# A two-layer graph attention kernel: the first stage's work dealt out anew over the engines

## The chip, the cores and the metric

The kernel runs on one core of a Trainium2 chip. The metric is the device time of one execution in microseconds (us), as the median of several runs. Five engines work side by side, each through its own queue of instructions in program order, and wait for each other by semaphores: TensorE (PE in the profile; PEld is its weight loads), VectorE (DVE), ScalarE (ACT), GpSimd (POOL) and SyncE (SP). SP and POOL here mostly issue DMAs.

## The reference

Two graph attention layers over 512 nodes, a residual and a layer norm. There are 16,896 edges (8,192 drawn ones, the same reversed, and a loop at each node), sorted by destination. Layer 1 has 8 heads of 768 features, layer 2 has one.

```python
def gat_layer(x, W, a_s, a_d, b, edge_index, concat):
    h = (x @ W).reshape(n, H, C)
    alpha_s = jnp.einsum('nhc,hc->nh', h, a_s)
    alpha_d = jnp.einsum('nhc,hc->nh', h, a_d)
    e = jax.nn.leaky_relu(alpha_s[src] + alpha_d[dst], 0.2)
    m = jax.ops.segment_max(e, dst, num_segments=n)
    e = jnp.exp(e - m[dst])
    denom = jax.ops.segment_sum(e, dst, num_segments=n)
    alpha = e / (denom[dst] + 1e-16)
    out = jax.ops.segment_sum(h[src] * alpha[:, :, None], dst, num_segments=n)
    return out.reshape(n, H * C) + b

h = elu(gat_layer(x, W1, a_src1, a_dst1, b1, edge_index, True))
y = gat_layer(h, W2, a_src2, a_dst2, b2, edge_index, True)
return layernorm(x + y)
```

## The kernel before

The edges become a dense matrix `cnt` of 512 by 512 (how often an edge runs from a source to a destination), in 4 tiles of 128 destinations. Each head is then dense: a projection of x, logits, a softmax of each tile over all 512 sources with the counts as weights, attention, ELU, and a product with the head's rows of W2 added into `h2`.

**The large products** are made of fewer, smaller ones (Strassen's way, by halves): seven products P1 to P7 of sums and differences of blocks, each in two parts i = 0, 1 with three steps each (`product`, L422). `left(xT, xS)` (L401) gives the sums of the transposed x: `s1` to `s4` on VectorE (L406 to L409). The weights' sums of head 0 are made by `weight_sums` (L554): one VectorE addition, `w1t` (L556), which P5 reads, and then accumulating DMAs of GpSimd: `t2 += t1` (L261), which P6 reads, one into `w1r` (L558), which P7 reads, and `t4 += t2` (L262), which P4 reads. The same function loads the weights of head 1 and makes their sums.

**The first stage** (not `general`, from L700) counts the edges beside the projection of head 0 (`first_projection`, L601, 14 items) and the first four items of head 1's (`projection`). The edges are in 132 chunks of 128. For each chunk a one-hot tile of its sources is made, on VectorE (L753) or, for tile 2 of the destinations, on ScalarE (L751); for each quarter of the chunks VectorE makes the destinations' side (`here`, `odw`, L731, L732); TensorE multiplies the two (L779) into one PSUM bank a tile. Sources are folded in half, and the counts of the two halves lie in one number as digits; `counted_in_digits` (L578) takes them apart: `higher` (ScalarE: `upper` and a half of `cnt`), `lower` (VectorE, the other half), `mask` (ScalarE, `absent`, from `cnt`).

The order is written out by hand. `batches` (L815) deals the chunks into nine batches, as pairs of numbers: so many of the other tiles' chunks, so many of tile 2's. In each batch VectorE gets the destinations of new quarters, then the one-hots, with what is `waiting` in their middle; then come the `extra` steps (L809), then the projection's items up to `wants[n]`, then the batch's counting. An item's addition on VectorE is put into `waiting`, and so comes in the middle of the next batch's one-hots. `logits(0, ...)` makes both halves of a tile's logits (L441): with the source vector `a_s`, then with the destination vector `a_d`.

In the last batch `spread` (L649) transposes and broadcasts the source logits of head 0 on TensorE. A tile's softmax steps are `lift` (ScalarE: logit sum, L669), `leak` (VectorE, L673), `rank` (VectorE: mask and maximum, L678; ScalarE: exponential, L684), then `give`: `weigh` (VectorE: L936 to L940), scale and a copy on ScalarE (L956, L959), a transposing DMA on SP (L961), and `turn_in` (ScalarE, L964) into `PT`.

**The rest of head 1's projection** is a loop over `pairs[4]` to `pairs[13]`, two each for P6, P7, P4, P5 and P3; P4 accumulates into P7's bank and waits for P7's addition (L465), P3 likewise into P5's. What is put between them stands in `beside` (L1158): the rest of head 0's softmax, `done[n]`, which empties a pair, and sums. `load_a(1)` loads head 1's two vectors into the tiles of head 0's.

**Head 0's attention** is `near_first` (L1056, matmuls L1067), whose last argument says which steps come beside which product, among them halves of head 1's logits and `row_out(1)` (DVE, then DMAs through DRAM that broadcast the source logits). Then follows `by_halves(h2, ...)`, head 0's part of the second layer, with the softmax of head 1 beside it. Heads 1 to 7 aren't touched otherwise.

Of the kernel before, what the change touches and what calls it, by code (L numbers as in the profile page):

```python
# [39 lines left out]
def gat_pass(  # L40
# [393 lines left out]
    def half_logits(h, t):  # L434
        return [lambda al=al, a=a, sign=sign: nc.vector.scalar_tensor_tensor(
            scr, HS[h][:, t, :], sign, a, op0=ALU.mult, op1=ALU.mult, accum_out=al[:, t:t + 1])
            for al, a, sign in zip(AL[h], A[h], (1.0, -1.0))]

    def logits(h, feats, t):
        for al, a, sign in zip(AL[h], A[h], (1.0, -1.0)):  # L440
            nc.vector.scalar_tensor_tensor(scr, feats[:, t, :], sign, a, op0=ALU.mult,  # L441
                                           op1=ALU.mult, accum_out=al[:, t:t + 1])
# [135 lines left out]
    def counted_in_digits(t, ps, steps):  # L578

        both = ps[:, :HN]  # L580
        if steps:
            st = ohp.tile([P, HN + 1], F32, name="steps")
            nc.scalar.activation(st[:, 1:], both, AF.Copy, scale=0.5)
            nc.scalar.activation(st[:, :1], ps[:, HN - 1:HN], AF.Copy, scale=-0.5)
            both = ohp.tile([P, HN], F32, name="both")
            nc.vector.tensor_tensor(both, st[:, 1:], st[:, :HN], op=ALU.subtract)
        upper = ohp.tile([P, HN], F32, name="upper", bufs=2)

        def higher():
            nc.scalar.activation(upper, both, AF.Identity, bias=minus_round, scale=-1.0)  # L590
            nc.scalar.activation(cnt[:, t, HN:], upper, AF.Copy, bias=-ROUND / DIGIT, scale=-1.0 / DIGIT)

        def lower():
            nc.vector.scalar_tensor_tensor(cnt[:, t, :HN], upper, ROUND, both, op0=ALU.add, op1=ALU.add)

        def mask():
            nc.scalar.activation(absent[:, t, :], cnt[:, t, :], AF.Relu, bias=far, scale=NO_EDGE)

        return higher, lower, mask
# [72 lines left out]
    def leak(q):  # L672
        nc.vector.scalar_tensor_tensor(q, q, NEG_SLOPE, q, op0=ALU.mult, op1=ALU.min)  # L673
# [37 lines left out]
    if not general:  # L711
# [46 lines left out]
        def sources(chunks, between):  # L758

            for j, c in enumerate(chunks):  # L760
                if j == len(chunks) // 2:
                    for f in between:
                        f()
                one_hot(c, False)
# [3 lines left out]
        def count(batch, rest):  # L768
# [14 lines left out]
            for t in range(NT):  # L783
                if t not in done and all(todo[b] == 0 for b in range(t * P // B, (t + 1) * P // B)):
                    higher, lower, mask = counted_in_digits(t, cps[t], t == S)
                    if n + 2 < len(batches):
                        higher()
                        waiting.append(lower)
                        masks.append(mask)
                    elif rest:  # L790
                        higher()
                        lower()
                        mask()
                    else:
                        deferred.extend([higher, lower, mask])
                    done.add(t)


# [7 lines left out]
        def ask():  # L806
            nc.vector.tensor_scalar(flag, pst[:1, :1], -1.0, float(E), op0=ALU.mult, op1=ALU.add)

        extra = {0: [inside], 1: [lambda: B1.update(weight_sums()), ask, s1, s2, s4], 3: [s3],  # L809
                 5: [lambda: logits(0, HS[0], 0)],  # L810
                 6: [lambda: logits(0, HS[0], 1), lambda: logits(0, HS[0], 2)], 7: [lambda: logits(0, HS[0], 3)]}
        B1 = {}
        wants = [3, 4, 7, 10, 12, 14, 16, 18]
        batches = []
        for ours, theirs in ((16, 0), (8, 8), (8, 8), (12, 4), (12, 4), (12, 4), (13, 3), (14, 2), (4, 0)):  # L815
            take = [order[k][:m] for k, m in ((False, ours), (True, theirs))]
            del order[False][:ours], order[True][:theirs]
            batches.append(take[0][:ours // 2] + take[1] + take[0][ours // 2:])
        assert not any(order.values())
        pos, made, quarter, waiting, masks = 0, set(), EC // NT, [], []  # L820
        for n, batch in enumerate(batches):
            fresh = sorted({c // quarter for c in batch} - made)
            made.update(fresh)
            if n == 0:
                waiting = [lambda k=k: destinations(k) for k in fresh]
            else:
                for k in fresh:
                    destinations(k)
            if n + 1 < len(batches):
# [34 lines left out]
            if n + 1 == len(batches):  # L864
                spread(0)
                q = [lift(0, t) for t in range(2)]
                for t in range(2):
                    leak(q[t])
                for f in deferred:
                    f()  # L870
                q += [lift(0, t) for t in range(2, NT)]
                leak(q[2])
                for t in range(NT - 1):
                    rank(q[t], t)
            if n == 0:
                pst = mm.tile([P, 512], F32, name="mm")
                nc.tensor.matmul(pst[:1, :1], found, ones, start=True, stop=True)
            if n == 3:
                again = nc.values_load(flag[:1, :1], min_val=0, max_val=E)
            count(batch, n + 1 == len(batches))  # L880
        assert not extra and not waiting and pos == len(items) and len(done) == NT
    else:
        for t in range(NT):
# [231 lines left out]
            behind = [others]  # L1115
        return behind[0]()

    load_a(1, a_src1[1], a_dst1[1])

    gF, xF = gT.rearrange("p c n -> p (c n)"), xS.rearrange("p a k n -> p (a k n)")  # L1120
    RELOAD = 5
# [27 lines left out]

    AA, lsums = left_sums(0)  # L1150
    BB, rsums = right_sums()
    some_logits, one_logits = half_logits(1, 2), half_logits(1, 3)

    def give(t):
        turn_out(q[t], t, weigh(q[t], t, scale=False))

    done = {n: (lambda n=n: pairs[n][1]()) for n in range(4, 13)}
    beside = {4: [lambda: give(0)], 5: [done[4]], 6: [done[5]], 7: [done[6], lambda: give(1)],  # L1158
              8: [done[7], lambda: leak(q[3]), lambda: rank(q[3], 3), lambda: turn_in(0)], 9: [lambda: give(2), done[8]],
              10: [lambda: give(3), lambda: turn_in(1), done[9]], 11: [done[10], lsums[0]],  # L1160
              12: [done[11], lambda: turn_in(2), *lsums[1:3]], 13: [done[12], lambda: turn_in(3), *one_logits[:1], *some_logits[:1]]}
    for n in range(4, 14):
        pairs[n][0]()
        for f in beside[n]:
            f()
        if n == 10:
            load_w2(0, "w1")()
            B2, pending = right(W2[0], "w1")
# [57 lines left out]
    for h in range(H - 1):  # L1226
# [13 lines left out]
        row = [lambda: row_out(h + 1)]  # L1240
        if h == 0:
            GA, gsums = left(gT, gS)
            finish = near_first(0, AA, BB, [*rsums, lsums[3]], {(0, 1): sources[:1], (1, 1): list(sources[1:]) + row, (2, 1): [some_logits[1], one_logits[1]]})
            load_w1(2)()
            load_a(2, a_src1[2], a_dst1[2])
            attend = attended(0)
# [8 lines left out]
            gsums[1]()  # L1255
            pending[0]()
            pairs[2][0]()
            targets[0]()
            gsums[2]()
            targets[1]()  # L1260
            pairs[3][0]()
# [8 lines left out]
            for n in range(2, 7):  # L1270
                (m0, e0), (m1, e1) = pairs[2 * n:2 * n + 2]
                m0()
                m1()
                if n == 3:
                    e0()
                if n < 6:
                    scored(n - 2)
                if n < 5:
                    score(n - 1)
                if n == 6:  # L1280
                    turn_in(0)
                    out_by_dma(2)
                if n != 3:
                    e0()
                if 3 < n < 6:
                    out_by_dma(n - 4)
# [303 lines left out]
```

## Time and profile before

| | |
|---|---|
| median of 3 runs | 627.65 us |
| the runs | 628.01, 625.67, 627.65 us |
| the profiled execution | 625.49 us |
| its span (first to last instruction) | 623.7 us |
| granted TensorE clock, mean | 0.996 |
| TensorE busy | 609.6 us |
| VectorE busy | 525.9 us |
| first stage and rest of head 1's projection | 0 to 78.15 us |
| head 0's attention | 78.15 to 96.28 us |
| head 0's part of layer 2 | 96.28 to 123.60 us |

The profile is of one execution. A row of the order in time has the start, the time from the first start to the last end, the engine, the line, the operation with its tiles, and in brackets how long the engine was idle before it and what ended that. A row of waits has the waiting engine, line and tile, what it waited for, and us in total, how often, and the longest.

### The profile page before, as it was taken

The numbers are of one execution on the slowest core, as the hardware profiler recorded it, in microseconds if no ns is written. First come the engines' busy times: TensorE is split into PE (matmuls) and PEld (weight loads), VectorE is DVE, ScalarE is ACT, GpSimd is POOL, SyncE is SP. The second block draws the span as 40 slices with busy tenths as digits, with TensorE's granted clock in tenths as the row PEclk, the third lists the DMA queues.
The fourth block names the chain that finished last, engine by engine and source line by source line (L and its number), as shares of the span: only waits on it lengthen the run. The fifth ranks groups of instructions, "written<-read, shape, count | busy, mean of one in ns | idle before, by whom it ended". The sixth has DMA issues, their size and how long they took to land.

```text
span 623.7 us, 8556 instructions
## 1 busy us (share of the span) xinstructions
PE 609.6 (98%) x2765; PEld 482.0 (77%) x2765; DVE 525.9 (84%) x1137; ACT 333.8 (54%) x607; POOL 150.6 (24%) x188
## 2 busy tenths in 40 slices
PE   8899899999999999999999999999999999999995
PEld 5555586556888888888888888888888888886553
DVE  8988889897899879977798779977898778978785
ACT  4655858640748146751758146751758146754361
POOL 2210011023342324323342333313342323010000
PEclk9999999999999999999999999999999999999998
DMA  8995398699999999999999998999999995690032
GB/s 291 334 230 120 70 263 270 173 252 260 237 216 142 319 250 215 171 294 213 250 217 178 301 261 206 168 274 217 250 218 180 318 284 96 115 260 17 17 77 79
DMA packets 109569, 129.46 MB, mean 208 GB/s; under 512 B 41622, under 2 KB 90446, under 8 KB 108750
## 3 DMA queue, kind: packets, MB, share of 16 engines
q1 hardware_dynamic: 75518, 91.35, 48.1%
q0 software_dynamic: 33568, 36.90, 38.6%
q10 hardware_dynamic: 432, 0.59, 0.3%
q8 instruction: 24, 0.39, 0.2%
q14 instruction: 27, 0.22, 0.1%
HBM read 99.84 MB, written 2.90 MB: 165 GB/s over the span
## 4 chain that ended last, share of the span: by engine, by line
PE 89%; DVE 8%; ACT 1%; issue 1%; DVEq 0%; ACTq 0%
PE mm L497 43%; PE mm L1027 17%; PE mm L426 16%; PE mm L1067 6%; PE mm L1536 3%; DVE os L753 2%; PE held L426 1%; DVE scr L441 1%; DVE h L510 1%; DVE q L673 1%; PE bc L278 1%; DVE q L678 0%; DVE odw L732 0%; ACT q L684 0%; DVE here L731 0%
## 5 line engine op out<-in xcount | busy, mean ns | idle before, releaser
L503 ACT ACTIVATE hs<-mm 128x512 f32<-128x512 f32 x30 | 17.9, 596 | 86.0 <-PE mm L497 85.4
L1027 PE MATMUL mm<-PT,hs 128*128 128x256 f32 x216 | 52.5, 379 | 0.0
L510 DVE TENSOR_TENSOR hs<-hs,mm 128x512 f32<-128x512 f32 x45 | 30.9, 686 | 22.2 <-PE mm L497 21.0
L682 ACT ACTIVATE q<-q,nmax 128x512 f32<-128x512 f32 x32 | 23.1, 721 | 49.3 <-DVE nmax L678 49.2
L508 POOL DMA_DIRECT2D h<-pass x22 | 26.5, 1319 | 85.7 <-ACT pass L507 85.7
L1027 PEld LDWEIGHTS mm<-PT,hs 128*128 128x128 f32 x216 | 41.1, 190 | 5.8
L510 DVE TENSOR_TENSOR h<-h,mm 128x512 f32<-128x512 f32 x56 | 38.3, 684 | 6.6 <-PE mm L497 5.5
L964 ACT COPY PT<-zr 128x1024 uint16<-128x1024 uint16 x34 | 39.3, 1156 | 5.0 <-DMA zr<-pS 4.5
L497 PE MATMUL mm<-w2r,xT 128*128 128x256 f32 x160 | 37.8, 379 | 0.0
L497 PE MATMUL mm<-w2r,gT 128*128 128x256 f32 x160 | 37.0, 379 | 0.0
L1027 PE MATMUL mm<-pS,gS 128*128 128x256 f32 x144 | 37.0, 379 | 0.0
L135 POOL DMA_DIRECT2D w1t<-in_L_gnn_W_dram x18 | 28.3, 1598 | 31.3 <-DVE gT L1132 28.2
L497 PE MATMUL mm<-w1r,hs 128*128 128x256 f32 x144 | 34.1, 380 | 0.2 <-DVE hs L1182 0.2
L497 PE MATMUL mm<-w1t,hs 128*128 128x256 f32 x144 | 34.1, 380 | 0.0
L497 PE MATMUL mm<-w1r,gS 128*128 128x256 f32 x144 | 34.0, 379 | 0.0
L497 PEld LDWEIGHTS mm<-w2r,gT 128*128 128x128 f32 x160 | 30.4, 190 | 4.1
L497 PEld LDWEIGHTS mm<-w2r,xT 128*128 128x128 f32 x160 | 30.4, 190 | 4.1
L497 PEld LDWEIGHTS mm<-w1r,hs 128*128 128x128 f32 x144 | 27.2, 190 | 4.2 <-DVE hs L1182 0.6
L497 PEld LDWEIGHTS mm<-w1t,hs 128*128 128x128 f32 x144 | 27.3, 190 | 3.9 <-ACT absent L507 0.2
L1027 PEld LDWEIGHTS mm<-pS,gS 128*128 128x128 f32 x144 | 27.4, 190 | 3.7
L497 PEld LDWEIGHTS mm<-w1r,gS 128*128 128x128 f32 x144 | 27.3, 190 | 3.6
L1031 ACT COPY u<-mm 128x256 f32<-128x256 f32 x18 | 6.7, 372 | 42.8 <-PE mm L1027 42.8
(308 smaller groups left out, 1573.2 us busy)
## 6 DMA issues: line engine op xcount, KB each, us to landing
w2r<-in_L_gnn_W_dram SPq DMA_DIRECT2D x48, 384.0 KB
w1r<-in_L_gnn_W_dram SPq DMA_DIRECT2D x43, 384.0 KB
gT<-xd SPq DMA_DIRECT2D x5, 1280.0 KB
w1t<-in_L_gnn_W_dram SPq DMA_DIRECT2D x24, 256.0 KB
h<-pass POOLq DMA_DIRECT2D x22, 256.0 KB, 4.9
w1t<-in_L_gnn_W_dram POOLq DMA_DIRECT2D x18, 256.0 KB, 6.1
w2t<-in_L_gnn_W_dram SPq DMA_DIRECT2D x15, 256.0 KB
w2t<-in_L_gnn_W_dram POOLq DMA_DIRECT2D x15, 256.0 KB, 9.0
```

The costliest lines, as they stand in the source:

```text
L135: nc.gpsimd.dma_start(o, i, accum_op=ALU.add)
L426: nc.tensor.matmul(ps[:, :HALF], A_[p][:, k, i * P:(i + 1) * P], B_[p][:, k, :], start=start and k == 0, stop=k == HK - 1, skip_group_chec ...
L497: nc.tensor.matmul(bank[chain][:, i * TH:(i + 1) * TH], A_[p][:, k, i * P:(i + 1) * P], B_[p][:, k, :], start=first and i == k == 0, stop= ...
L503: nc.scalar.activation(out(o), ps, AF.Copy, scale=sign)
L508: nc.gpsimd.dma_start(out(o), part, accum_op=ALU.add)
L510: nc.vector.tensor_tensor(out(o), out(o), ps, op=ALU.add if sign > 0 else ALU.subtract)
L682: nc.scalar.activation(q, q, AF.Exp, bias=nmax, scale=-1.0, accum_out=dens[t])
L753: nc.vector.tensor_scalar(o, nodes[:, :HN], low[:, c:c + 1], None, op0=ALU.is_equal)
L964: nc.scalar.copy(PT.rearrange("p s n -> p (s n)").bitcast(U16).rearrange("p (s n h) -> p s n h", s=NT, h=2)[:, :, t * P:(t + 1) * P, :], p ...
L1027: nc.tensor.matmul(bank[p][:, :HN], A_[p][:, k, c * P:(c + 1) * P], B_[p][:, k, :], start=over is None and k == 0, stop=k == 1, skip_group ...
L1067: nc.tensor.matmul(banks[c, p][:, :HN], A_[p][:, k, c * P:(c + 1) * P], B_[p][:, k, :], start=over is None and k == 0, stop=k == 1, skip_g ...
L1536: nc.tensor.matmul(ps[:, :cols.stop - cols.start], PT[:, s, t * P:(t + 1) * P], h2[:, s, cols], start=(s == 2), stop=(s == 1))
```

## The change

Nothing of the computation changes. The order does:

- The weight sum, the flag and `s1` come ahead of batch 1's destinations and one-hots; the addition of P2's first part and `inside` come at the end of batch 0. From batch 1 on, the first of what is `waiting` is put ahead of the batch's destinations.
- The batches are dealt a little differently, and batches 1 and 2 take two P5 products and two P3 products.
- Head 0's logits are dealt out in halves: all source halves by batch 6, then two destination halves, and the last one (tile 3) beside head 1's P7. In the last batch only tiles 0 and 1 are ranked; the counting's last part comes before that. Tiles 2 and 3 follow beside P7, and their transposes go back to back (0 with 1, 2 with 3).
- `upper` lies in the bytes of the tile's own `absent`.
- `load_a(1)` is issued behind the first P7 product. One half of head 1's logits goes from before attention into it, `row_out(1)` from the second group of products to the third; two destination halves go into head 0's part of layer 2, and one comes out.

```diff
+    def half(t, j, h=0):
+        return lambda: half_logits(h, t)[j]()
...
-        upper = ohp.tile([P, HN], F32, name="upper", bufs=2)
+        upper = absent[:, t, :].bitcast(F32)
...
-                if j == len(chunks) // 2:
+                if j == len(chunks) // (4 if n == 5 else 2):
...
-                    elif rest:
-                        higher()
-                        lower()
-                        mask()
                     else:
-                        deferred.extend([higher, lower, mask])
+                        deferred.append((higher, lower, mask))
...
-        extra = {0: [inside], 1: [lambda: B1.update(weight_sums()), ask, s1, s2, s4], 3: [s3],
-                 5: [lambda: logits(0, HS[0], 0)],
-                 6: [lambda: logits(0, HS[0], 1), lambda: logits(0, HS[0], 2)], 7: [lambda: logits(0, HS[0], 3)]}
+        ahead_of = {1: [lambda: B1.update(weight_sums()), ask, s1]}
+        extra = {1: [s2, s4], 3: [s3], 5: [half(0, 0), half(0, 1), half(1, 0)],
+                 6: [half(2, 0), half(3, 0)], 7: [half(1, 1), half(2, 1)]}
...
-        wants = [3, 4, 7, 10, 12, 14, 16, 18]
+        wants = [3, 6, 8, 10, 12, 14, 16, 18]
...
-        for ours, theirs in ((16, 0), (8, 8), (8, 8), (12, 4), (12, 4), (12, 4), (13, 3), (14, 2), (4, 0)):
+        for ours, theirs in ((16, 0), (6, 8), (8, 8), (13, 4), (13, 4), (13, 4), (13, 3), (13, 2), (4, 0)):
...
             else:
+                first = ahead_of.get(n, [])
+                for f in waiting[:1] + first:
+                    f()
+                del waiting[:1]
                 for k in fresh:
                     destinations(k)
...
             if n + 1 == len(batches):
                 spread(0)
                 q = [lift(0, t) for t in range(2)]
-                for t in range(2):
-                    leak(q[t])
-                for f in deferred:
-                    f()
-                q += [lift(0, t) for t in range(2, NT)]
-                leak(q[2])
-                for t in range(NT - 1):
-                    rank(q[t], t)
+                count(batch, True)
+                (higher, lower, mask), last_tile = deferred
+                leak(q[0])
+                higher()
+                q.append(lift(0, 2))
+                rank(q[0], 0)
+                leak(q[1])
+                lower()
+                mask()
+                rank(q[1], 1)
             if n == 0:
+                waiting.pop()()
+                inside()
...
-    load_a(1, a_src1[1], a_dst1[1])
...
-    beside = {4: [lambda: give(0)], 5: [done[4]], 6: [done[5]], 7: [done[6], lambda: give(1)],
-              8: [done[7], lambda: leak(q[3]), lambda: rank(q[3], 3), lambda: turn_in(0)], 9: [lambda: give(2), done[8]],
-              10: [lambda: give(3), lambda: turn_in(1), done[9]], 11: [done[10], lsums[0]],
-              12: [done[11], lambda: turn_in(2), *lsums[1:3]], 13: [done[12], lambda: turn_in(3), *one_logits[:1], *some_logits[:1]]}
+    higher, lower, mask = last_tile if not general else [lambda: None] * 3
+    score_last = [] if general else [half(3, 1), lambda: q.append(lift(0, 3))]
+    rank_third = [] if general else [lambda: leak(q[2]), lambda: rank(q[2], 2)]
+    beside = {4: [lambda: give(0), done[4], lambda: give(1)], 5: [done[5]], 6: [done[6], *score_last, higher, *rank_third[:1]],
+              7: [done[7], *rank_third[1:], lower, mask, lambda: turn_in(0), lambda: leak(q[3]), lambda: rank(q[3], 3)],
+              8: [lambda: give(2), done[8], lambda: give(3)], 9: [done[9]],
+              10: [done[10], lambda: turn_in(1)], 11: [lambda: turn_in(2), done[11], lsums[0]],
+              12: [*lsums[1:3], lambda: turn_in(3), done[12]], 13: [half(3, 0, 1)]}
...
+        if n == 6:
+            load_a(1, a_src1[1], a_dst1[1])
...
-            finish = near_first(0, AA, BB, [*rsums, lsums[3]], {(0, 1): sources[:1], (1, 1): list(sources[1:]) + row, (2, 1): [some_logits[1], one_logits[1]]})
+            finish = near_first(0, AA, BB, [*rsums, lsums[3]], {(0, 1): [half(2, 0, 1)], (1, 1): sources[:1], (2, 1): [*sources[1:], *row, targets[0]]})
...
-            targets[0]()
...
-                if n == 3:
+                if n in (3, 5):
                     e0()
                 if n < 6:
                     scored(n - 2)
+                if n in (3, 4):
+                    half(n - 1, 1, 1)()
...
-                if n != 3:
+                if n not in (3, 5):
                     e0()
```

## The prediction

> **What bounds the kernel now.** I read the page's busy times first, then TensorE's waits over the whole run, then the order in time of TensorE and VectorE from 0 to 125 us, then GpSimd's DMAs there.
>
> ```profile
> span 623.7 us, 8556 instructions
> PE 609.6 (98%) x2765; PEld 482.0 (77%) x2765; DVE 525.9 (84%) x1137; ACT 333.8 (54%) x607; POOL 150.6 (24%) x188
> ...
> PE mm L426 <- DVE hs L465: 1.9, 1, 1.9
> PE mm L426 <- DVE xS L406: 1.8, 1, 1.8
> PE bc L278 <- DVE zeros L273: 1.3, 1, 1.3
> PE tr L652 <- DVE scr L441: 0.8, 1, 0.8
> PE held L426 <- DVE hs L621: 0.7, 1, 0.7
> PE mm L311 <- ACT xT L312: 0.2, 1, 0.2
> PE mm L877 <- ACT xT L312: 0.2, 1, 0.2
> PE mm L497 <- DVE hs L1182: 0.2, 1, 0.2
> ```
>
> TensorE is the bound: 609.6 of 623.7 us. Of the waits that the profile names, only 0.2 us lies behind the first stage (L497). In front of it four waits on VectorE add up to 5.26 us; here they are in order of time, with the start of attention (L1067) as the end mark.
>
> ```profile
> 19.92 4.14 PE L426 MATMUL mm<-w1t,xS 128*128 128x384 f32 x12 [1.80 <-DVE xS L406]
> ...
> 39.45 4.14 PE L426 MATMUL held<-w1t,xT 128*128 128x384 f32 x12 [0.73 <-DVE hs L621]
> ...
> 55.64 0.32 PE L652 MATMUL tr<-ident,wide 128*128 128x128 f32 x1 [0.79 <-DVE scr L441]
> ...
> 66.43 4.14 PE L426 MATMUL mm<-w2t,xT 128*128 128x384 f32 x12 [1.94 <-DVE hs L465]
> ...
> 78.15 3.62 PE L1067 MATMUL mm<-PT,hs 128*128 128x256 f32 x16
> ```
>
> The change adds and removes no matmul, so it can win at most these 5.26 us. VectorE and GpSimd at the same places:
>
> ```profile
> 17.59 1.34 DVE L556 TENSOR_TENSOR w1t<-w1r 128x1152 f32<-128x1152 f32 x1
> 18.86 0.14 DVE L807 TENSOR_SCALAR flag<-mm 1x1 int32<-1x1 f32 x1
> 18.93 0.94 DVE L406 TENSOR_TENSOR xS<-xT 128x768 f32<-128x768 f32 x1
> ...
> 63.56 0.42 DVE L594 SCALAR_TENSOR_TENSOR cnt<-upper,tr 128x256 f32<-128x256 f32 x1 [1.15 <-ACT upper L590]
> ...
> 65.83 0.55 DVE L465 TENSOR_TENSOR hs<-hs,mm 128x384 f32<-128x384 f32 x1
> ```
> ```profile
> 19.26 1.05 POOL L261 DMA_DIRECT2D w1t<-w1t  x1 [11.08 <-DVE flag L807]
> ...
> 28.23 0.91 POOL L262 DMA_DIRECT2D w1t<-w1t  x1 [6.58 <-DMA w1t<-w1t]
> ```
>
> The weight sum and the x difference that product P5 needs come behind 26 one-hot tiles and two quarters of destinations, at 17.6 and 18.9. At 63.56 VectorE waits for ScalarE, which does three exponentials (1.95 us) ahead of tile 3's upper digits. The last two lines are the accumulating DMA that makes P6's weights: issued 19.26, landed 28.23 (9.0 us), and P6 ran at 28.96.
>
> **How the parts were costed.** I wrote out both orders engine by engine and walked them with the mean start-to-start times of this trace: one-hot 0.196 us, a quarter of destinations 1.99, weight sum 1.27, x difference 0.97, a half of a tile's logits 1.00, leak 0.61, rank 0.70, weigh with reciprocal 1.0, an add out of PSUM 0.46; on TensorE 1.94 a product, 0.036 a counting matmul. For the old order the walk puts the fourth wait's end at 66.1 (trace 66.43), attention at 77.7 (78.15) and head 2's first product at 123.3 (123.60). For the new order it gives:
>
> *P5, 1.80 us.* After batch 0's one-hots (12.4): the add of P2 12.8 to 13.3, the two "inside" steps to 13.7, the sum to 15.0, the flag at 15.2, x difference done 16.3. TensorE wants it behind the second P2 product, which began at 15.10 in the trace: 17.0. The wait goes, 0.7 us to spare. Behind it 8 one-hots and a quarter end at 19.9; batch 1's counting starts after both P5 products at 20.9. The fourth x sum ends at 21.8, when P3 wants it: level within 0.1 to 0.5. The sum reads a weight half whose landing the trace doesn't show before 17.59; landed by 14.2 it costs nothing, at 17.6 it costs 3.4. By bytes (3.5 MB queued up to it, moved by 13 us at the rates of the profile's windows) I take nothing.
>
> *P4 of head 0, 0.73 us.* The two adds of P7 go from behind 6 one-hots to the head of batch 5 and behind its third: done at 35.0 and 38.0, wanted at 36.7 and 38.6. The wait goes. The adds and lower digits that now head batches 4, 5 and 6 hold up the one-hots queued behind them on VectorE, and with them the counting, if their product is late; in the walk none of the three is late.
>
> *Spread, 0.79 us.* The source logits of all four tiles end by 48.0, the transposes come at 51.0. Two ops less lie ahead of batch 7 and one (tile 3's destination half) goes behind the counting. The wait goes.
>
> *P4 of head 1, 1.94 us.* TensorE arrives at 59.8. VectorE now runs leak and rank of tile 0, of tile 1, then both weighings with the adds between: the P7 add ends at 60.3. Left: 0.55, and 0.13 at the second product. Tiles 2 and 3 are ranked beside P5 and P3, whose adds wait behind them: 0.41 more. ScalarE's last turn-in (74.2 against 78.6) then starts the sums that attention's P6 needs at 76.3, done 75.6; 0.31 is lost on a copy of ScalarE. The new waits make 1.40.
>
> *Logits of head 1, the a_s/a_d load, row_out.* One half (1.0 us) moves from before attention to behind it: attention keeps four halves, the second product of head 0 gets two for one. In the trace the add at 111.18 to 111.73 releases the product at 111.78: no room. But the half taken out lies in front of it, so the walk has the waits there at 0.2 us, as before. The load of head 1's vectors now waits on SP for tile 3's half (61.3), behind transposes 0 and 1 and ahead of 2 (68.1); wanted 72.3. row_out is 6 us later against TensorE, and load_w1(2) queues behind it on SP: its lift is reached 4.7 us after the row's broadcast is issued. The broadcast's landing isn't shown: at 3 us (estimate from the DMA transposes, 3.1) free, at 7 us it costs 1.3. I take nothing. load_w1(2)'s last accumulation was issued at 103.7; with the slowest landing of a GpSimd DMA up to 60 us, 15.1, it is in at 118.8, and wanted at 135: 6 us later still fits.
>
> *Upper digits in the mask's own tile.* Same two operations in order on ScalarE, which has to run upper before mask anyway: nothing; lost cover would cost its 0.4 us.
>
> **Sum.** Waits removed 5.26, new waits between 0 and 1.40 (TensorE does 1.0 us more work in the trace than in the walk up to there, so it reaches them later and part of them closes): 3.9 to 5.3, I take 4.5. Up to head 2 the walk keeps 4.9 of the 5.2 it had at attention, so the later stages give nothing back. The profiled execution took 625.49 us (span 623.7), so 621.0 for its like; the median of the runs is 2.16 higher, which the change doesn't touch: 627.65 - 4.5 = 623.1.
>
> **Rivals.** *The gain is mostly eaten by DMA:* P6 comes at 27.0 instead of 28.96, its accumulation is issued at 15.0 instead of 19.26. With the 8.7 to 9.5 us of the two such DMAs it lands by 24.5 and costs nothing. With the 13.9 us that L558's took, issued 0.8 us behind it in the same flood, it lands at 28.9: 1.9 lost, 2.6 left, 625.0. The late weight half or the row can do the same. For it: DMA engines at 1.0 of their time from 10 to 45 us. Against: both accumulations took 9.
>
> The Trainium skill (DMA: Bandwidth & Descriptors, Anatomy of one DMA) gives such a DMA some 2.0 us and its bytes at 436 GB/s. For 576 KB that would be an estimated 3.4 us and the sum unchanged; the trace's 9 us decides, since this queue isn't empty. The Trainium skill (SBUF — State Buffer, SBUF: two separate sides) speaks against moving the issue ahead of the one-hots: VectorE in a two-port mode locks GpSimd out while it writes descriptors. By that rule the landing would slip by up to the run of 8 one-hots, 1.6 us, still ahead of P6. The trace does not agree so far: an issue at 50.81 beside 19 one-hots took 0.86 us, one at 44.76 0.89.
>
> *Slower:* one mechanism, the same accumulation held until the old issue time because its other operand lands no earlier, and as slow as the slowest GpSimd DMA of the stage, 15.1 us: it lands at 34.4, TensorE stands 7.4 us at P6 and VectorE behind the P6 add, net 2.9 slower, 630.5. It decides from a landing of 31.5 on.
>
> *It doesn't do what it says:* VectorE is busy 8.9 of 10 us from 40 to 50, and the freed time reappears as waits of TensorE on counting or on attention's sums; within 1.5 us of before, about 626.5. For it: VectorE, not TensorE, ends all four waits. Against: the walk leaves VectorE's work before the spread one op shorter, and its idle spots in batches 4 to 6, 3.5 us in the trace, shrink to 1.2.
>
> **Chances.** Forecast 0.75; gain eaten 0.12; no effect 0.07; slower 0.06. Over 0.5% (3.1 us, about what a measurement of this kernel can tell from no change) faster means below 624.5: 0.75. The two middle cases are "same", 0.19. The range runs from 620.2 (5.3 off the profiled time) to 626.5 (the no-effect case).
>
> **What would show it.** Right: TensorE's list of waits without L406, L621 and L652, and L465 under 0.8 us; head 0's first P5 directly behind the second P2; attention starting near 73.5 and head 2's first product near 119. Wrong: a TensorE wait on a DMA of w1t in front of P6; VectorE waiting at L556; long waits of VectorE on L590 or L621; head 1's lift waiting for q from DRAM; a start of attention at 76 or later.

## The result and the profile after

The changed kernel takes 625.27 us, the median of 22 runs (622.68 to 628.07). The kernel before took 627.29 us beside it (22 runs, 625.49 to 628.35). The ratio is 0.9974, interval 0.9962 to 0.9986: 2.0 us faster at the medians, where 4.5 were forecast, and 0.26% by the ratio, less than the 0.5% that the prediction counts as a change. The runs of before lie in two groups, ten at 625.49 to 626.01 and twelve at 627.28 to 628.35; the experiments explain the gap. Beside the experiments below the kernel before was run again, with medians of 627.62 to 627.96, so a difference of some 0.7 us between the medians of two experiments says little.

The profiled execution after took 625.87 us (span 624.1), the one before 625.49 (623.7). So the two traces are of equal length, and the question is where the waits removed came back. The page of the kernel after, its span and busy times, and then TensorE's waits over the whole run (engine, tile and line that wait, releaser: us in total, times, longest):

```profile
span 624.1 us, 8551 instructions
PE 611.6 (98%) x2765; PEld 483.4 (77%) x2765; DVE 525.1 (84%) x1137; ACT 333.6 (53%) x607; POOL 150.7 (24%) x188
...
PE mm L426 <- ACT hs L465: 2.5, 1, 2.5
PE bc L278 <- DVE zeros L273: 1.3, 1, 1.3
PE held L426 <- issue: 0.7, 1, 0.7
PE held L426 <- DMA w1t<-w1t: 0.6, 1, 0.6
PE mm L426 <- ACT os L754: 0.4, 1, 0.4
```

Line numbers shift between the kernels: the changed kernel's L465 is P1's copy out of PSUM on ScalarE (L462 before), and before's L465, the addition of P7 on VectorE, is its L468. The four waits on VectorE are gone, that one included. There is a new wait on a DMA, one put down to "issue", and one of 2.5 us on a ScalarE copy. TensorE is busy 2.0 us longer than before with as many matmuls, so some of them ran slower. TensorE's order in time after:

```profile
17.60 4.03 PE L426 MATMUL mm<-w1t,xS 128*128 128x384 f32 x12
...
28.57 4.14 PE L426 MATMUL held<-w1t,xS 128*128 128x384 f32 x12 [0.60 <-DMA w1t<-w1t]
...
34.36 4.11 PE L426 MATMUL held<-w1r,xT 128*128 128x384 f32 x12 [0.73 <-issue]
...
39.11 4.14 PE L426 MATMUL held<-w1t,xT 128*128 128x384 f32 x12
...
74.49 3.62 PE L1075 MATMUL mm<-PT,hs 128*128 128x256 f32 x16
...
119.74 4.03 PE L426 MATMUL mm<-w2r,xT 128*128 128x384 f32 x12
126.30 5.81 PE L426 MATMUL mm<-w2r,xT 128*128 128x384 f32 x12 [2.53 <-ACT hs L465]
```

These rows give the account by place, before less after. P5 starts 2.32 us earlier (19.92 to 17.60), P6 0.39 (28.96 to 28.57), P4 of head 0 0.34 (39.45 to 39.11), attention 3.66 (78.15 to 74.49), head 2's first products 3.86 (123.60 to 119.74). The next two products of head 2 then wait 2.53 us and take 5.81 instead of 4.1. At head 1's attention the kernel is 0.6 behind before (151.30 against 150.69), and from there the traces agree. So the change won 3.9 us up to head 2's first product and lost 4.5 in the next ten us. What did it, first in VectorE's and GpSimd's rows of the front:

```profile
15.01 1.36 DVE L559 TENSOR_TENSOR w1t<-w1r 128x1152 f32<-128x1152 f32 x1 [0.58 <-DMA w1r<-in_L_gnn_W_dram]
16.35 0.93 DVE L406 TENSOR_TENSOR xS<-xT 128x768 f32<-128x768 f32 x1
```
```profile
18.78 1.15 POOL L261 DMA_DIRECT2D w1t<-w1t  x1 [9.97 <-DMA w1t<-in_L_gnn_W_dram]
...
28.81 0.91 POOL L262 DMA_DIRECT2D w1t<-w1t  x1 [7.53 <-DMA w1t<-w1t]
```

The weight sum comes 2.6 us earlier, after 0.58 us of waiting for the half `w1r`. The accumulation that P6 needs comes only 0.48 us earlier (19.26 before): it now waits for its other operand, the raw block `w1t` from DRAM, issued at 9.43 and landed at 18.15. It lands at 28.53, 9.7 us after its issue, and P6 starts at 28.57.

Then the chain of waits at the junction to head 2, in order of time:

```profile
112.75 0.33 SPq L224
...
115.42 5.86 DMA zr<-pS
121.28 0.02 issue
121.30 1.16 ACT PT L972
...
125.87 0.39 ACT hs L465
126.25 0.04 issue
126.30 8.72 PE mm L426 x21
```

It is read from the bottom. TensorE waits for a PSUM bank that ScalarE empties (L465). That copy stands in ScalarE's queue behind the softmax of tiles 2 and 3, and this behind `turn_in` of tile 0 (L972), which waits for tile 0's transposing DMA: 5.86 us. Before, the same DMA went from 119.16 to 122.27, 3.1 us, and ScalarE waited 0.60. SP's rows of the kernel before, and then of the one after, show what changed around it:

```profile
94.77 0.40 SPq L111 DMA_DIRECT2D w2t<-in_L_gnn_W_dram  x1
...
105.68 0.33 SPq L224 DMA_DIRECT2D a_d<-in_L_gnn_a_dst_dram  x1
106.11 0.39 SPq L1199 DMA_DIRECT2D w2t<-in_L_gnn_W_dram  x1
...
119.16 3.77 SPq L961 DMA_TRANSPOSE zr<-pS  x2
```
```profile
97.15 0.40 SPq L111 DMA_DIRECT2D w2t<-in_L_gnn_W_dram  x1
...
112.75 0.33 SPq L224 DMA_DIRECT2D a_d<-in_L_gnn_a_dst_dram  x1
113.18 0.37 SPq L1211 DMA_DIRECT2D w2t<-in_L_gnn_W_dram  x1
...
115.42 10.01 SPq L969 DMA_TRANSPOSE zr<-pS  x3
```

Two groups of loads slid towards the transpose. Head 2's weights (L111 and on, and two accumulating DMAs of GpSimd behind them) are queued behind `row_out(1)`, which now comes a group of products later: 2.4 us later on the clock, 6 against TensorE. The loads of `attended(0)` (L1211 to L1214, 1,152 KB) are queued behind the load of `a_d` (L224), which overwrites a tile that the last destination half of head 1's logits still reads. That half has moved into the second product, so SP stands there until 112.75, and its four loads end at 115.30, right at the issue of the transpose; before, they were out 11 us ahead of it.

The DMA packets show which of the two the transpose met here. In the kernel before, its 1,056 packets, all under 512 B, move from about 120.35 us on, 1.2 us after the issue. In the changed kernel only 57 packets of that size move in the 3.7 us between the issue and 119.15 us. The other packets that SP's queue moves until then, 1.1 MB, are larger: the loads issued just ahead. So nearly all of the delay is a later start behind them. Head 2's weights were not beside the transpose: their last accumulation, issued at 106.27, landed 9.2 us later, at 115.5, and from 116 us on GpSimd's queue moved nothing.

### The profile page after: what moved, and what is told of

Same layout as the page of the kernel before. It is cut to its first block, busy times and chain, and to the rows that moved or that the text cites. A ratio compares the mean times of both kernels' runs of the same rounds, so it can differ in the third digit from the quotient of the medians.

```text
span 624.1 us, 8551 instructions
## 1 busy us (share of the span) xinstructions
PE 611.6 (98%) x2765; PEld 483.4 (77%) x2765; DVE 525.1 (84%) x1137; ACT 333.6 (53%) x607; POOL 150.7 (24%) x188
## 4 chain that ended last, share of the span: by engine, by line
PE 89%; DMA 5%; DVE 3%; ACT 1%; issue 1%; SPq 0%; DVEq 0%; ACTq 0%; POOLq 0%
PE mm L500 46%; PE mm L1035 17%; PE mm L426 13%; PE mm L1075 6%; PE mm L1549 3%; PE held L426 2%; DMA w1t<-w1t 2%; DMA w1t<-in_L_gnn_W_dram 1%; DMA zr<-pS 1%; DVE scr L435 1%; PE tr L782 1%; DMA w1r<-in_L_gnn_W_dram 1%; DMA hs<-in_x_dram 1%; DVE q L681 0%; DVE cnt L698 0%
## 5 line engine op out<-in xcount | busy, mean ns | idle before, releaser
L972 ACT COPY PT<-zr 128x1024 uint16<-128x1024 uint16 x34 | 39.3, 1155 | 6.4 <-DMA zr<-pS 5.3
```

The lines of the kernel that those rows point to most:

```text
L972: nc.scalar.copy(PT.rearrange("p s n -> p (s n)").bitcast(U16).rearrange("p (s n h) -> p s n h", s=NT, h=2)[:, :, t * P:(t + 1) * P, :], p ...
```

## Experiments

**The two loads at the junction, each alone.** The first kernel puts the loads of `attended(0)` ahead of the vector load, in the second the weights go ahead of `near_first` and so ahead of `row_out(1)`:

```diff
             load_w1(2)()
-            load_a(2, a_src1[2], a_dst1[2])
             attend = attended(0)
+            load_a(2, a_src1[2], a_dst1[2])
```


> The changed kernel with head 2's two vector loads issued on SP behind the three loads of attended(0) instead of ahead of them. Theory (SP's order): the vector load waits until 112.75 for head 1's last destination half, the 1.1 MB behind it start at 113.2 and share the DMA engines with tile 0's transpose at 115.42, which then takes 5.9 us instead of 3.1; ScalarE waits 2.5 us for it ahead of the copy of head 2's first product, TensorE stands 2.5 us, and its granted clock is halved for the next 3.4 us (1.8 us more). Expected: transpose landing in about 3.1 us, no TensorE wait over 0.5 us at head 2's second product, granted clock 1.0 from 120 to 130 us, 4.3 us less than the changed kernel, median near 621. Rival (the later row_out, which delays the load of head 2's weights, fills the DMA engines): transpose still over 5 us, wait and time as in the changed kernel, near 625.

Measured: 624.28 us (12 runs, 622.44 to 626.22), ratio to before 0.9954 [0.994, 0.9968]. The loads of `attended(0)` went out at 99.8 to 103.6. The transposing DMA still took 5.3 us (114.15 to 119.5) and TensorE waited 1.9 us instead of 2.5 (the profile is of the fastest of the twelve runs, 622.44). The theory is half right: these loads were not the only ones. Moved forward, they held up the rest. The last accumulation of head 2's weights now took 13.7 us to land instead of 9.2, until 118.5, and from 114.15 to 116.85 us GpSimd's queue and SP's, with the vector loads in it, kept the engines busy together.

```diff
+            load_w1(2)()
             finish = near_first(0, AA, BB, [*rsums, lsums[3]], {(0, 1): [half(2, 0, 1)], (1, 1): sources[:1], (2, 1): [*sources[1:], *row, targets[0]]})
-            load_w1(2)()
```


> The changed kernel with the load of head 2's weights issued on SP ahead of head 0's attention, and so ahead of row_out. Rival theory (the delayed weight load is what loads the DMA engines at 115 us): the transpose of head 1's tile 0 lands in about 3 us, the wait at head 2's second product goes, near 621. Theory (SP's order of the vector load): the 1.1 MB still start at 113 us just ahead of the transpose; wait and halved clock stay in good part, within 1.5 us of the changed kernel's 625.3.

Measured: 626.50 us (12 runs, 624.78 to 629.97), ratio 0.9998 [0.9979, 1.0017]. TensorE's waits in that run:

```profile
PE mm L426 <- ACT hs L465: 2.7, 1, 2.7
PE mm L426 <- DVE h L468: 1.9, 2, 1.4
```

The weights alone repair nothing. They were in long before: from 114 to 116 us the DMA engines were busy for only 0.10 of the time. But the loads of `attended(0)` still went out at 115.2 to 117.3, right ahead of the transpose, which took 6.1 us. The second line is a new wait: `row_out`'s broadcast was issued only at 100.12, 6.1 us after its writes began (2.25 before), and ScalarE's first lift of head 1 waited 3.1 us for it.

**Both loads early.** The rest of the change stays; the row and one source half go back to their old groups, which lets the weights go early, and `attended(0)` comes ahead of the vector load. The two destination halves stay in the second product:

```diff
-              12: [*lsums[1:3], lambda: turn_in(3), done[12]], 13: [half(3, 0, 1)]}
+              12: [*lsums[1:3], lambda: turn_in(3), done[12]], 13: [half(3, 0, 1), half(2, 0, 1)]}
...
-            finish = near_first(0, AA, BB, [*rsums, lsums[3]], {(0, 1): [half(2, 0, 1)], (1, 1): sources[:1], (2, 1): [*sources[1:], *row, targets[0]]})
+            finish = near_first(0, AA, BB, [*rsums, lsums[3]], {(0, 1): sources[:1], (1, 1): [*sources[1:], *row], (2, 1): [targets[0]]})
             load_w1(2)()
-            load_a(2, a_src1[2], a_dst1[2])
             attend = attended(0)
+            load_a(2, a_src1[2], a_dst1[2])
```


> The changed kernel with both loads brought forward: half of tile 2's source logits back ahead of attention and row_out back beside the second group of products, so that head 2's weights are issued near 91 us, and the three loads of attended(0) ahead of the two vector loads. The two destination halves stay in head 0's part of layer 2. Theory: as x5, transpose about 3.1 us, no wait at head 2's second product, median 621 to 622. Rival (the two halves in the second product cost VectorE time that TensorE waits for): waits of TensorE on L468 of over 1 us in sum, median near 623 to 624.

Measured: 622.39 us (6 runs, 621.70 to 624.02), ratio 0.9915 [0.9889, 0.9941], and no wait of TensorE at head 2. Here are the windows that hold tile 0's transposing DMA, in the kernel before, after, with `attended(0)` alone early, and with both early. Behind the window's length the columns are TensorE, its weight loads, VectorE, ScalarE and GpSimd in busy us (and instructions), the granted clock, the busy share of the DMA engines, and GB/s:

```profile
119.20:122.30 3.10, 3.10 (x10) 1.63 (x9) 1.80 (x7) 2.47 (x5) 0.00 (x0) 1.00 0.44 85
```
```profile
115.40:121.30 5.90, 5.90 (x19) 3.43 (x19) 3.92 (x14) 2.47 (x4) 0.00 (x0) 1.00 1.03 294
```
```profile
114.20:119.50 5.30, 5.30 (x18) 3.10 (x17) 3.32 (x13) 2.47 (x4) 0.00 (x0) 1.00 1.06 250
```
```profile
115.80:119.20 3.40, 3.40 (x12) 1.98 (x11) 2.53 (x11) 2.37 (x4) 0.00 (x0) 1.00 0.43 88
```

The transposing DMA takes 3.1 to 3.4 us when the DMA engines are at 0.44 of their time, and 5.3 to 6.1 us in the three kernels that have them full. The four kernels make a table of two by two: both loads late, 2.53 us of waiting; `attended(0)` early alone, 1.90; weights early alone, 2.69; both early, none. The last cell is not a pure one, since the row and one half moved back with the weights. Either load late was enough, so both must be out of the way.

**Head 1's part undone.** Here the last item of the change is taken back (halves of head 1's logits, the row, the order in the second product), all but the place of `load_a(1)`, and the first stage stays as changed:

```diff
-              12: [*lsums[1:3], lambda: turn_in(3), done[12]], 13: [half(3, 0, 1)]}
+              12: [*lsums[1:3], lambda: turn_in(3), done[12]], 13: [half(3, 0, 1), half(2, 0, 1)]}
...
-            finish = near_first(0, AA, BB, [*rsums, lsums[3]], {(0, 1): [half(2, 0, 1)], (1, 1): sources[:1], (2, 1): [*sources[1:], *row, targets[0]]})
+            finish = near_first(0, AA, BB, [*rsums, lsums[3]], {(0, 1): sources[:1], (1, 1): [*sources[1:], *row], (2, 1): [half(2, 1, 1), half(3, 1, 1)]})
...
             pairs[2][0]()
+            targets[0]()
             gsums[2]()
...
-                if n in (3, 5):
+                if n == 3:
                     e0()
...
-                if n in (3, 4):
-                    half(n - 1, 1, 1)()
...
-                if n not in (3, 5):
+                if n != 3:
                     e0()
```


> The changed kernel with head 1's logits, row_out and the order of head 0's second product as before: only the first stage and the rest of head 1's projection are changed. Theory (both loads that SP delays, head 2's weights behind row_out and attended(0) behind the vector load, meet tile 0's transpose at 114 to 118 us; each alone is enough, which is why x1 and x2 moved little): here neither is late, the transpose lands in about 3.1 us, TensorE doesn't wait at head 2's second product, granted clock 1.0 from 120 to 130 us; attention starts 0.2 to 1 us later than in the changed kernel for the one half more ahead of it, head 2's first product at 119.5 to 120.5, median near 622. Rival (the transpose is late because everything of head 0 comes 4 us earlier against the DMAs): transpose over 5 us, a wait over 1.5 us, median near 625.

Measured: 622.01 us (6 runs, 621.48 to 623.22), ratio 0.991 [0.9886, 0.9935]. ScalarE's row of `turn_in`, first of the changed kernel and then of this one:

```profile
121.30 1.16 ACT L972 COPY PT<-zr 128x1024 uint16<-128x1024 uint16 x1 [2.47 <-DMA zr<-pS]
```
```profile
117.83 1.16 ACT L972 COPY PT<-zr 128x1024 uint16<-128x1024 uint16 x1 [0.63 <-DMA zr<-pS]
```

The DMA takes 3.1 us (114.70 to 117.83), and TensorE does not wait. So without head 1's part the change is worth 5.3 us at the medians (627.29 to 622.01), and head 1's part costs 3.3 (625.27 less 622.01), more than the 2.5 us of its wait. In the profiles attention comes 5.4 us earlier than before (72.75), head 2's first product 4.5 (119.14), and the end 4.0 (621.48 against 625.49).

**The clock behind the wait.** The rest is in the windows behind the wait; here TensorE's granted clock is the third column from the right. In the changed kernel:

```profile
126.00:128.00 2.00, 1.70 (x3) 1.10 (x4) 2.00 (x3) 1.69 (x3) 0.00 (x0) 0.58 0.87 165
128.00:130.00 2.00, 2.00 (x4) 0.98 (x4) 1.04 (x2) 0.00 (x0) 0.00 (x0) 0.57 0.98 81
130.00:132.00 2.00, 2.00 (x8) 1.19 (x7) 0.00 (x0) 1.54 (x2) 0.14 (x1) 1.00 1.12 351
```

From 126 to 130 us it is about half, and TensorE gets through 4 matmuls in 2 us instead of 8. This kernel fills the gap with four matmuls that nothing reads:

```diff
             for n in range(14):
+                if n == 2:
+                    fill = bc.tile([P, 512], F32, name="bc")
+                    for _ in range(4):
+                        nc.tensor.matmul(fill[:, :HALF], ident, xT[:, 0, :HALF], start=True, stop=True)
                 pairs[n][0]()
```


> The changed kernel with four matmuls of 128x384 whose result nobody reads put between head 2's two P1 products and its P2 (2.6 us of TensorE work in the place of the 2.5 us wait). Theory (an idle TensorE loses half its clock afterwards): granted clock stays 1.0 from 126 to 130 us, P2's two products take 4.0 instead of 5.8 us, 1.8 us less than the changed kernel, near 623.5. Rival (P2 is slow because its weight rows arrive late): the two products still take 5.8 us and the time stays at 625 or above.

Measured: 623.66 us (6 runs, 623.59 to 624.56), ratio 0.9947 [0.993, 0.9965], 1.6 us below the changed kernel. The same windows, with the two products in 4.14 us instead of 5.81:

```profile
126.00:128.00 2.00, 2.00 (x7) 1.14 (x6) 2.00 (x3) 1.15 (x2) 0.00 (x0) 1.00 0.84 145
128.00:130.00 2.00, 2.00 (x8) 1.20 (x7) 0.15 (x1) 1.60 (x3) 0.00 (x0) 1.00 0.88 274
```

The idle spell costs twice: 2.5 us itself, and 1.7 at half the clock. The Trainium skill (TensorE: Matmul & The Clock Gate, Part 1: The HAM clock gate) lets the clock fall to a half after at least one idle window of about 3.4 us, counted by a window that runs freely. The run differs in the length, and the measurement decides: 2.53 us were enough here. That the phase matters agrees in kind: in the profiles of other kernels of this study idle spells of 1.90, 1.94, 2.69 and 2.78 us left the clock at 1.0. The window itself no run here shows.

**The same in the kernel before.** Before waits 1.94 us at head 1's P4 (L465). If its upper group of runs are those in which the clock falls there, three matmuls in that gap must do away with the group:

```diff
     for n in range(4, 14):
+        if n == 8:
+            fill = bc.tile([P, 512], F32, name="bc")
+            for _ in range(3):
+                nc.tensor.matmul(fill[:, :HALF], ident, xT[:, 0, :HALF], start=True, stop=True)
         pairs[n][0]()
```


> The kernel before with three matmuls of 128x384, whose result nobody reads, ahead of head 1's P4, where TensorE waited 1.94 us for L465. Nothing else is changed. Theory (the runs of before lie in two groups, near 625.7 and near 627.8, because that wait takes half the clock afterwards in about half of the runs): all runs near 625.7, median 2 us below before's. Rival (the two groups come from elsewhere, DMA landings or the end): still two groups, median near 627.5.

Measured: 626.00 us (12 runs, all between 625.44 and 626.63), ratio 0.9973 [0.9959, 0.9986]. The upper group is gone. The half clock itself was not seen in before, whose profile is of the lower group. But each run's mean granted clock is on record: of the 61 runs of before beside the experiments, the 23 up to 626.80 us have 0.9973 on average, the 38 from 627.49 us on 0.9951. The difference, 0.0022 of some 625 us, is 1.4 us at full clock, most of the 2 us between the groups. So the filled gap and these means both speak for the clock; where in the run it falls, the filled gap alone shows.

**The front alone.** Before, with only the weight sum, the x difference and the new deal of the batches:

```diff
-        extra = {0: [inside], 1: [lambda: B1.update(weight_sums()), ask, s1, s2, s4], 3: [s3],
+        ahead_of = {1: [lambda: B1.update(weight_sums()), ask, s1]}
+        extra = {1: [s2, s4], 3: [s3],
...
-        wants = [3, 4, 7, 10, 12, 14, 16, 18]
+        wants = [3, 6, 8, 10, 12, 14, 16, 18]
...
-        for ours, theirs in ((16, 0), (8, 8), (8, 8), (12, 4), (12, 4), (12, 4), (13, 3), (14, 2), (4, 0)):
+        for ours, theirs in ((16, 0), (6, 8), (8, 8), (13, 4), (13, 4), (13, 4), (13, 3), (13, 2), (4, 0)):
...
             else:
+                for f in ahead_of.get(n, []):
+                    f()
...
             if n == 0:
+                waiting.pop()()
+                inside()
```


> The kernel before with only the front of the first stage changed: inside and P2's first addition at the end of batch 0, weight sum, flag and x difference ahead of batch 1, the new deal of chunks and the two P5 and two P3 products in batches 1 and 2. Theory (DMA landings bind P6 and P7): the 1.8 us wait at P5 goes, but P6 and P7 of head 0 still start at 28.6 and 34.0 to 34.4, attention still near 78, time within 0.3 us of before. Rival (the prediction's step): attention 1.8 us earlier, 625.5.

Measured: 625.59 us (12 runs, 624.59 to 627.00), ratio 0.998 [0.9967, 0.9993]. In order of time:

```profile
27.53 4.14 PE L426 MATMUL held<-w1t,xS 128*128 128x384 f32 x12 [0.46 <-DMA w1t<-w1t]
33.36 4.11 PE L426 MATMUL held<-w1r,xT 128*128 128x384 f32 x12 [0.77 <-issue]
```

The L406 wait of 1.80 is gone, these two appear, and the waits at L621, L652 and L465 stay (0.61, 0.7, 1.93). Head 2's first product is 0.9 us earlier than before, and so is the end of the profiled execution (624.59 against 625.49). It lies between the theory and the rival: half of the 1.80 us survives. The median (1.7 us below 627.29) is no better measure of it, since the wait at L465 is still there, and with it the chance of the half clock.

**The operand of the accumulation earlier.** In the changed kernel the raw operands of the sums go out on SP ahead of the third load of `w1r`:

```diff
-    for r, ks in ((0, slice(0, 1)), (0, slice(1, HK)), (1, slice(0, HK))):
+    for r, ks in ((0, slice(0, 1)), (0, slice(1, HK))):
         nc.sync.dma_start(W1[0][r][:, ks, R], block(w1_0, r, R)[:, ks])
...
     B0, additions0 = sums_by_dma(W1[0], w1_0, "w1")
+    nc.sync.dma_start(W1[0][1][:, :, R], block(w1_0, 1, R))
```


> The changed kernel with the two loads that feed head 0's accumulated weights issued on SP ahead of the load of the block that P3 reads. Theory (P6 and P7 of head 0 are bound by when GpSimd can start its two accumulations, and that by the landing of this load at 18.2 us): GpSimd's first accumulation issued 1 to 1.5 us earlier, P6 without a wait on w1t, P7 at about 33 instead of 34.4, attention at 73.3 instead of 74.5; the end differs by at most that and by the wait at head 2's second product, median near 624.3. Rival (the DMA engines are full until 45 us, so the order of loads only moves the landing): P7 still at 34.0 to 34.4.

Measured: 624.38 us (10 runs, 622.31 to 626.26), ratio 0.9946 [0.9928, 0.9965]. GpSimd's and TensorE's rows, one line number higher here:

```profile
17.03 1.05 POOL L261 DMA_DIRECT2D w1t<-w1t  x1 [8.86 <-DMA w1t<-in_L_gnn_W_dram]
```
```profile
27.71 4.14 PE L427 MATMUL held<-w1t,xS 128*128 128x384 f32 x12
...
32.70 4.14 PE L427 MATMUL held<-w1r,xT 128*128 128x384 f32 x12
```

The accumulation is issued 1.75 us earlier and lands at 26.1; P6 and P7 no longer wait, and attention starts at 72.86 instead of 74.49. The wait on w1t varies between runs (0.5 to 0.6 us in four of the profiles without this edit, none in three), but each of those has 0.3 to 0.8 us in front of P7, and neither kernel with the edit has any. So P7's wait too comes from the DMAs of the front. At the medians the edit is worth 0.9 us, hardly more than the 0.7 us by which the medians of before differ; the earlier P6, P7 and attention are what shows it. The wait at the junction stays (2.78 us).

**Both repairs.** The two edits above together, head 1's part undone and the operand earlier:

> x5 (head 1's logits, row_out and the second product's order as before) and x7 (the operands of head 0's accumulated weights loaded first) in one kernel. Theory: the two repairs sit in different places and add up as far as the DMA landings of a run allow: no wait of TensorE at P6 and P7 of head 0 and none at head 2's second product, 0.3 to 1 us below x5's 622.0, so 621.0 to 621.7. Rival (in x5 the accumulations start early enough, 17.4 us against 18.8 in the changed kernel, so that loading them first brings nothing more): 622.0 as x5.

Measured: 621.28 us (6 runs, 621.00 to 622.77), ratio 0.9909 [0.9889, 0.9929], the fastest version here, 6.0 us below the 627.29 of before. No wait at P6, P7 or head 2 is left. Over the kernel with head 1's part undone it gains 0.7 us, within the spread of the runs of both; attention starts at 72.82 against 72.75 in that kernel's profile, whose landings in front happened to be early (0.3 us waited at P7). Whether the second repair adds to the first stays open.

## Why the prediction was right, and where it was wrong

The four waits went as forecast, and the time was lost again elsewhere. The step that failed is the one on head 1's logits, the a_s/a_d load and `row_out`: it was put at nothing and cost some 3.3 us. A smaller part, 1.75 us, came back in front, as waits that the P5 step had not counted. That the measured 625.27 lies within the stated range, and next to the 625.0 of "mostly eaten by DMA", is luck, since most of the loss came at a place that neither rests on.

*P5, 1.80 us*: the wait went, as said; that the time would stay won was wrong. The step took the second weight half as landed. It held up VectorE by 0.58 us, which was slack for P5, but is part of why the x sum that P3 reads ended at 22.76, where the walk has 21.8. And the step took P6's accumulation as issued at 15.0. It was issued at 18.78, since the raw operand lands at 18.15. That is the condition of the rival *slower*; its price, a landing after 15.1 us, did not come, the landing took 9.7. P7's load was the other slip: in before, L558's 13.9 us from an issue at 20.04 end at 33.94, and P7 starts at 34.02, with no slack to give. No step weighed that landing against P7. So the 1.80 came back as 0.42 at P3 (the place called level within 0.1 to 0.5; the profile names ScalarE there, but TensorE starts 0.1 us after that x sum), 0.60 at P6 and 0.73 at P7.

*P4 of head 0, Spread, P4 of head 1*: right. All three waits are gone; where 0.55 and 0.13 were allowed to remain at L465, nothing did. From head 0's P4 to head 1's the lead grows from 0.34 to 3.55 us. Attention came 3.66 us earlier, at 74.49, where the mark was 73.5.

*Logits of head 1, the a_s/a_d load, row_out*: this is the term that sank the forecast. "I take nothing" should have been some 3.3 us, by the kernel with this part undone. The step asked of each late load whether its own reader could wait, and for the weights that was true: they were in at 115.5, inside the 118.8 worked out, and wanted at 135. For `row_out`'s broadcast a price of nothing was right, too: TensorE does not wait at L468. It did not ask which other transfer would meet these loads, and the transposing DMA of tile 0 is issued at 115.42. And it did not look at what stands behind the `a_d` load on SP, the 1,152 KB of `attended(0)`, behind which the transpose then started late: 5.86 us instead of 3.1, a wait of 2.53 us, and 1.7 us at half the clock. "The later stages give nothing back" fell with it.

*The sum*: it took the profiled time as the start and added the 2.16 us to the median as something "which the change doesn't touch". By the kernel before with its gap filled, these 2 us are the clock after the wait at L465, and removing that wait removes them too. With the junction repaired the medians fall by 4.9 to 6.0 us, more than the 4.5 forecast; some 2 of these are the clock, which leaves some 3 to 4 for the waits. In the changed kernel itself the clock falls at the junction instead, in most of its runs: their mean granted clock is 0.993 to 0.997 in 18 of 22, and 0.998 in the others, among them the three fastest.

*The rivals*: "mostly eaten by DMA" named the right resource and its mark, a TensorE wait on a DMA of w1t in front of P6, appeared; but it looked at P6, and the larger part was eaten at 121 us. "Slower" had the right condition and the wrong price. Of the marks named, attention near 73.5 (74.49) and head 2's first product near 119 (119.74) came within a microsecond; "L465 under 0.8" held, since the addition it means has no wait left (the 2.5 us at L465 after are head 2's copy on ScalarE, another line). The issue at 50.81 that the prediction sets beside 19 one-hots lasts 0.86 us, time for only four of them, so it says less about that rule than it seems to. No mark was set for what lies behind head 2's first product, where the time went.

## What to carry to other kernels

A step that moves takes everything queued behind its waits with it: for each load that slides, ask not only when its own reader wants it, but which latency-bound transfer will now stand behind or beside it. A stall removed ahead of a product that a DMA releases is only worth the slack of that DMA, so check the operands of the accumulation and not just the engine that issues it. Here an idle spell of TensorE of 2 to 2.5 us could cost nearly as much again in clock, not every time, and three or four matmuls that nobody reads did away with that.

## What the hardware showed that was not expected

- The transposing DMA took 3.1 to 3.4 us on quiet DMA engines and 5.3 to 6.1 when they were full. In the changed kernel its packets came only as those of the loads issued ahead on SP's queue ran out, at 119.15 us. The Trainium skill (DMA: Bandwidth & Descriptors, Queues, rings and completion order) lets each DMA engine go round the queues that have work, packet by packet. The kernel with `attended(0)` alone early agrees in kind: from 114.15 to 116.85 us SP's queue and GpSimd's both had work, and their packets took 0.50 and 0.62 of the engines' time. In the changed kernel only SP's queue was left by 116 us.
- The accumulation of 576 KB for P6 landed 9.7 us after its issue, the 576 KB into `w1r` beside it 14.7, both with the DMA engines full (a busy share of 1.06 and 1.07).
- The granted clock fell to a half after 2.53 us of idling (0.65, 0.50, 0.50 and 0.64 in the four windows of 1 us from 126 us on). The kernel before has runs in two groups 2 us apart, and filling one idle spell of 1.94 us did away with the upper one.
